# Fewer table loads on ScalarE, silus of a pair of places together, and attention steps of unequal spacing in a macaron block

## The chip, the cores and the metric

The kernel runs on one core of one Trainium2 chip. The core has five engines with an instruction queue each: TensorE (PE in the profile; its weight loads are listed as PEld), VectorE (DVE), ScalarE (ACT), GpSimd (POOL) and SyncE (SP), which here only issues transfers. The metric is the device time of one execution in microseconds (us), lower is better.

## What is computed

Eight sequences of 512 tokens with 512 channels go through half a feed-forward network, attention, and half a feed-forward network again, each behind a layer norm and added to its input:

```
x = x + 0.5 * ffn(layernorm(x), w_gate, w_up, w_down)
x = x + attn(layernorm(x), W_q, W_k, W_v, W_o)
x = x + 0.5 * ffn(layernorm(x), w_gate, w_up, w_down)
```

`ffn` has 2048 hidden channels. Of every four neighbours of `silu(x @ w_gate) * (x @ w_up)`, only the two of largest magnitude are kept; then comes `@ w_down`. `attn` has 16 query heads and 4 key and value heads of 32 channels, with rotary positions on queries and keys, and a softmax over the 512 keys. All of it is in 32-bit floats.

## The kernel before

**Tiles and stages.** The 16 feed-forward blocks (8 sequences, first and second half) are the main stream. Each goes through four chunks `c` of 512 hidden channels, and each chunk through two places (`pair`), one for gate and up of 256 hidden channels. A place is done by `woven`: seven products of half size (Strassen's scheme) in place of eight, named by their PSUM banks x, v and z. Each product is four matmuls in the program and eight in the profile, some 1.73 us of PE (starts 0.216 us apart). Partial results are collected in the SBUF tiles `row` and `corner`; `copied` puts a first partial result there by ACT or by DVE, whichever the planner takes to be free sooner. Silu of the gate part and the multiply by the up part are done for three pieces: the corner (line 634, after the fifth product), the part still in x (line 645) and the row (line 650), both after the last product. Each multiply is recorded as a small task for DVE.

After two places `keep_two_of_four` masks the chunk: `magnitudes` takes the absolute values of one half on ACT (line 371), DVE compares them and multiplies (lines 384 to 409), POOL makes five sums for the products that follow (lines 415 to 420). Those seven products, with the banks y, are `products` (line 523); they are held in `owed` and given out between later places.

**Attention and layer norms are side stages.** They are Python generators. Between two products of the main stream, at most one step of each running side is issued. An attention is 65 steps: the layer norm (loads, moments on DVE, scales on POOL at lines 272 to 280, four `normalise` on ACT at line 283, four transposes), five projections and V, then, for four groups `c` of heads, scores and their maxima (line 805, reduced on DVE), their transpose, and for each of four key tiles `st` and the exponential p (lines 838 to 846), and `ops`, which multiplies p by V (line 854). p is added up over key tiles on DVE; `den` (line 872) sums it over keys, and the reciprocal is made on ACT as exp(-ln(den)) (lines 875 and 877). At the end come four products with W_o (line 932).

**What sets the order.** The schedule is written by the kernel itself: instructions run on each engine in the order in which the Python code records them. A planner keeps an estimated time for PE, DVE and ACT in `at`, and `takes` advances it. DVE tasks wait in three queues (`urgent`, `put_off`, `for_later`), and `fill`, called after a group of matmuls, records those that fit before the estimated time of PE; otherwise it takes a step of the masking. `ensure` records a task that something needs now. A side has a first and a last place, and its steps are due at equal distances between them (`pace`); a step is issued when its due place is past and its `ready` time has come, or it is three places late.

**Tables.** ACT's function tables are loaded by an instruction of their own. The build puts one ahead of an activation whose function isn't in the table that is loaded. `function(f)` runs f on a dummy of one column, so that the load happens there and not in front of the data:

```
    def function(f):
        nc.scalar.activation(dummy[:, 1:2], dummy[:, 0:1], f)
        takes("act", 1.4)
```

It is called for Exp before each p and for Silu after each p, and for Silu after each reciprocal. Ln and the Exp of the reciprocal have no such call, and their loads stand at their own lines.

Of the kernel before, what the change touches and what calls it, by code (L numbers as in the profile page):

```python
# [26 lines left out]
def macaron_block(  # L27
# [98 lines left out]
    ones32 = const.tile([P, HD], FP, name="ones32")  # L126
    nc.vector.memset(ones32, 1.0)
    dummy = const.tile([P, 2], FP, name="dummy")
    nc.vector.memset(dummy, 0.0)

    z = const.tile([P, NT, N_KV, HD], BF, name="z")
    nc.vector.memset(z, 0.0)
# [87 lines left out]
    def copied(dst, src):  # L220
# [5 lines left out]
        nc.vector.tensor_copy(dst, src)  # L226
        return takes("dve", 0.62, pe_heard())

    def function(f):

        nc.scalar.activation(dummy[:, 1:2], dummy[:, 0:1], f)  # L231
        takes("act", 1.4)

    def transposed(parts):

# [111 lines left out]
    def fill(slack=HEARD):  # L347

        while True:
            steps = thin["next"]  # L350
            for queue in (urgent, put_off, for_later):
                if queue and queue[0].fits(slack):
                    queue[0].run()
                    break
            else:
                if not steps or max(at["dve"], steps[1]) + steps[0] > at["pe"] + slack:
                    return
                step()

# [3 lines left out]
    def keep_two_of_four(h, made, sums=None, halves=(0, 1)):  # L363

        thin["halves"] = halves[0]

        def magnitudes(half):
            a = sp.tile([P, 4, HALF], FP, tag="a", name="a")  # L370
            nc.scalar.activation(a, h[:, :, half * HALF : (half + 1) * HALF], AF.Abs)  # L371
            takes("act", 1.06, at["dve"])
            return a

        yield 0.0, at["pe"] + 2.0
        ensure(made)
        a = magnitudes(halves[0])
        for half in halves:
            hh = h[:, :, half * HALF : (half + 1) * HALF]
            yield 0.7, at["act"]  # L380

            m = sp.tile([P, 8, HALF], BF, tag="m", name="m")
            g01, g23, g02, g13, g03, g12, s0, s1 = (m[:, i, :] for i in range(8))
            nc.vector.tensor_tensor(m[:, 0:2, :], a[:, 0:4:2, :], a[:, 1:4:2, :], ALU.is_ge)
            yield 0.72, 0.0
            nc.vector.tensor_tensor(m[:, 2:4, :], a[:, 0:2, :], a[:, 2:4, :], ALU.is_ge)
            yield 0.7, 0.0
            nc.vector.tensor_tensor(g03, a[:, 0, :], a[:, 3, :], ALU.is_ge)
            nc.vector.tensor_tensor(g12, a[:, 1, :], a[:, 2, :], ALU.is_ge)  # L389
            if half != halves[-1]:  # L390
                a = magnitudes(half + 1)

            yield 0.4, 0.0
            nc.vector.tensor_tensor(s0, g01, g02, ALU.add)
            nc.vector.tensor_tensor(s1, g12, g13, ALU.add)
            yield 0.4, 0.0
            nc.vector.tensor_tensor(s0, s0, g03, ALU.add)
            nc.vector.tensor_tensor(s1, s1, g01, ALU.subtract)
            yield 0.4, 0.0
            nc.vector.tensor_tensor(g02, g02, g12, ALU.add)  # L400
            nc.vector.tensor_tensor(g03, g03, g13, ALU.add)
            yield 0.4, 0.0
            nc.vector.tensor_tensor(g02, g23, g02, ALU.subtract)
            nc.vector.tensor_tensor(g03, g03, g23, ALU.add)
            for r, (s, op, n) in enumerate(
                ((s0, ALU.is_ge, 2.0), (s1, ALU.is_ge, 1.0), (g02, ALU.is_ge, 0.0), (g03, ALU.is_le, 1.0))
            ):
                yield 0.36, 0.0
                nc.vector.scalar_tensor_tensor(hh[:, r, :], s, n, hh[:, r, :], op, ALU.mult)  # L409
            if sums is not None:  # L410


                (h11, h21), (h12, h22) = ([h[:, i::2, :HALF], h[:, i::2, HALF:]] for i in range(2))
                if half == 0:
                    nc.gpsimd.tensor_tensor(sums[:, 2], h11, h12, ALU.add)  # L415
                else:
                    nc.gpsimd.tensor_tensor(sums[:, 1], h21, h22, ALU.add)  # L417
                    nc.gpsimd.tensor_tensor(sums[:, 0], h11, h22, ALU.add)
                    nc.gpsimd.tensor_tensor(h12, h12, h22, ALU.subtract)
                    nc.gpsimd.tensor_tensor(h21, h21, h11, ALU.subtract)  # L420
            thin["halves"] = half + 1

    def step():
        us, ready = thin["next"]
        thin["next"] = next(thin["steps"], None)
        takes("dve", us, ready)

    def need(halves):
        while thin["halves"] < halves and thin["next"]:
# [64 lines left out]
    def ffn(b, final, last):  # L494
# [68 lines left out]
        def hidden(h, i, r, cols):  # L563

            n = cols.stop - cols.start
            for m in range(2):
                ps = Bank([P, n], "gu")
                for k in range(ND):
                    w = quarters[(b, final), i, ((Q11, Q12), (Q21, Q22))[r % 2][k // 2]]
                    nc.tensor.matmul(  # L570
                        out=ps.tile, lhsT=w[:, m, k % 2, :], rhs=xT[:, k, cols], start=(k == 0), stop=(k == ND - 1)
                    )
                takes("pe", 3.62 * n / S)
                fill()
                if m == 0:
                    nc.scalar.activation(h[:, r, cols], ps.tile, AF.Silu)
                    ps.free(end=takes("act", 0.6, pe_heard()))
                else:
                    nc.vector.tensor_tensor(h[:, r, cols], h[:, r, cols], ps.tile, ALU.mult)
                    ps.free(end=takes("dve", 0.62, max(pe_heard(), at["act"])))  # L580
                yield n / S

        def woven(h, i, r, last_one):
# [47 lines left out]
            yield 0.5  # L631
            product(x, S3, ts[:, 2], False, end)
            end = add(corner, x, at_corner)
            nc.scalar.activation(h[:, r + 1, HALF:], corner[:, 0, :], AF.Silu)
            takes("act", 0.4, end)
            multiply = partial(nc.vector.tensor_tensor, h[:, r + 1, HALF:], h[:, r + 1, HALF:], corner[:, 1, :], ALU.mult)
            corner_slots.used(later(0.36, multiply, at["act"]))
            yield 0.5
            z = Bank([P, 2, HALF], "z")
            product(z, Q12, b21, True)  # L640
            at_left = add(left, z, 0.0)
            z.free(end=at_left)
            yield 0.5
            product(x, Q22, ts[:, 3], False, end)
            nc.scalar.activation(h[:, r + 1, :HALF], x.tile[:, 0, :], AF.Silu)
            takes("act", 0.38, pe_heard())
            multiply = partial(nc.vector.tensor_tensor, h[:, r + 1, :HALF], h[:, r + 1, :HALF], x.tile[:, 1, :], ALU.mult)
            last_one[:] = [soon(0.36, multiply, at["act"])]
            x.free(last_one)
            nc.scalar.activation(h[:, r, :], row[:, 0, :], AF.Silu)  # L650
            takes("act", 0.62, at_left)
            multiply = partial(nc.vector.tensor_tensor, h[:, r, :], h[:, r, :], row[:, 1, :], ALU.mult)
            last_one += [row_slots.used(later(0.65, multiply, at["act"]))]
            yield 0.5

        def combine_gu(i):
# [83 lines left out]
    def attention(b):  # L740
# [92 lines left out]
        def exponentials(c, t, mT):  # L833

            st = sc_slots.tile([P, N_KV, S], FP, "st")
            p = p_slots.tile([P, N_KV, S], FP, "p")
            for kv, rows in enumerate(heads):
                nc.tensor.matmul(  # L838
                    out=st[:, kv, :], lhsT=kT[rows, t * P : (t + 1) * P], rhs=qT[rows, c, :], start=True, stop=False
                )  # L840
            for kv in range(N_KV):
                rows = slice(kv * HD, kv * HD + 3)
                nc.tensor.matmul(out=st[:, kv, :], lhsT=ones[rows, :], rhs=mT[rows, :], start=False, stop=True)
            takes("pe", 1.45)
            function(AF.Exp)
            nc.scalar.activation(p, st, AF.Exp)  # L846
            end = takes("act", 1.88, max(pe_heard(), p_slots.ready + 0.1))
            function(AF.Silu)
            return p, end

        def weighted(t, ops, p):
# [15 lines left out]
        def divided(c, ops, p, sums):  # L867
# [4 lines left out]
                nc.tensor.matmul(out=den.tile[rows, :], lhsT=ones32, rhs=p[:, kv, :], start=True, stop=True)  # L872
            takes("pe", 1.6)
            rT = w_slots.tile([P, S], FP, "rT")
            nc.scalar.activation(rT, den.tile, AF.Ln)
            den.free(end=takes("act", 1.9, pe_heard()))
            nc.scalar.activation(rT, rT, AF.Exp, scale=-1.0)
            takes("act", 1.95)
            function(AF.Silu)
            made = later(0.65, partial(nc.vector.tensor_tensor, qT[:, c, :], ops, rT, ALU.mult), at["act"])  # L880
            return [acc_slots.used(w_slots.used(made))]

# [68 lines left out]
    normed = {(b, i): {} for b in range(B) for i in range(2)}  # L951
    WIDTH = 7 * NCH + 7 * NCH // 2
    NORM = 5 + 2 * NT
    ATTENTION = NORM + ND + 2 + NT + 1 + ND * (2 * NT + 1) + 1 + NT

    def place(b, i):
# [26 lines left out]
    def start():  # L983
        for side in list(sides):
            first, last, steps, stage, needs, name = side
            if first <= n and needs in past:
                sides.remove(side)
                pace = (last - first) / steps
                running.append({"due": first, "pace": pace, "left": steps, "stage": stage(), "ready": now})
                running[-1]["name"] = name  # L990

    def go_on(side):

        side["left"] -= 1
        side["due"] += side["pace"]
        side["ready"] = next(side["stage"])
        fill()
        if not side["left"]:
# [76 lines left out]
```

## Time and profile before

| what | us |
|---|---|
| median of 3 runs (3311.47 to 3315.4) | 3312.73 |
| the profiled execution | 3314.09 |
| its span, first to last instruction | 3312.3 |
| ACT: exponentials p, 128 of 1.867 | 238.9 |
| ACT: table loads at line 231, 290 of 1.283 | 372.1 |
| ACT: table loads at lines 875 and 877, 32 each | 41.1 and 41.1 |
| ACT: absolute values, 128 of 1.053 | 134.8 |
| DVE: maxima of scores, 512 of 0.683 | 321.6 |
| DVE: sums and quotients of p by line 157, 384 of 0.717 | 254.7 |
| POOL: five kinds of sums after the masking, 62 each | 414.5 |

The span is one execution under the profiler; the medians come from executions without it. A row of a group of instructions gives line, engine, operation, output and inputs with shapes, the count, busy time, mean ns of one, and how long the engine was idle just before them and for whom it waited. A table of waits gives the waiting engine, instruction and line, what it waited for, and the total, the number and the longest wait. In a table of stretches, the figures after each window are its length, the busy times of PE, PEld, DVE, ACT and POOL with counts, the granted clock of PE, the busy share of the DMA engines, and GB/s.

### The profile page before, as it was taken

The numbers are of one execution on the slowest core, as the hardware profiler recorded it, in microseconds if no ns is written. First come the engines' busy times: TensorE is split into PE (matmuls) and PEld (weight loads), VectorE is DVE, ScalarE is ACT, GpSimd is POOL, SyncE is SP. The second block draws the span as 40 slices with busy tenths as digits, with TensorE's granted clock in tenths as the row PEclk, the third lists the DMA queues.
The fourth block names the chain that finished last, engine by engine and source line by source line (L and its number), as shares of the span: only waits on it lengthen the run. The fifth ranks groups of instructions, "written<-read, shape, count | busy, mean of one in ns | idle before, by whom it ended". The sixth has DMA issues, their size and how long they took to land.

```text
span 3312.3 us, 43741 instructions
## 1 busy us (share of the span) xinstructions
PE 3224.5 (97%) x15880; PEld 2322.0 (70%) x15880; DVE 2293.9 (69%) x4949; ACT 1368.8 (41%) x1841; POOL 569.4 (17%) x868
## 2 busy tenths in 40 slices
PE   8899999999999999999999999998999999999999
PEld 6787657765677667766776668765676668765786
DVE  6767865686577775777668865787568765786554
ACT  2222662246424562266324652256425552266221
POOL 0222002210130022111121112120120122101120
PEclk9999999999999999999999999999999999999999
DMA  7563333542344435334453345333533436333451
GB/s 254 186 234 102 109 120 119 175 140 96 116 165 140 131 116 185 127 120 132 142 171 123 121 142 193 128 113 104 189 103 131 140 123 205 100 122 118 138 172 48
DMA packets 249285, 463.21 MB, mean 140 GB/s; under 512 B 24432, under 2 KB 64368, under 8 KB 248304
## 3 DMA queue, kind: packets, MB, share of 16 engines
q1 hardware_dynamic: 249072, 460.42, 42.3%
q8 instruction: 127, 2.08, 0.3%
q14 instruction: 86, 0.70, 0.1%
HBM read 421.53 MB, written 38.80 MB: 139 GB/s over the span
## 4 chain that ended last, share of the span: by engine, by line
PE 84%; DVE 8%; ACT 4%; DMA 2%; issue 1%; POOL 1%; SPq 0%; DVEq 0%; ACTq 0%; POOLq 0%
PE x L594 22%; PE y L523 21%; PE v L594 11%; PE z L594 6%; PE proj L760 4%; PE sc L805 4%; PE ops L854 4%; PE st L838 4%; PE y L932 3%; DMA xn<-x 1%; PE tr L239 1%; PE gu L570 1%; ACT p L846 1%; PE den L872 1%; DVE p L157 1%
## 5 line engine op out<-in xcount | busy, mean ns | idle before, releaser
L594 PE MATMUL x<-ts,w 128*128 128x256 f32 x3000 | 726.3, 385 | 12.0 <-ACT row L224 6.5
L594 PEld LDWEIGHTS x<-ts,w 128*128 128x128 f32 x3000 | 562.1, 191 | 170.9 <-issue 55.7
L523 PE MATMUL y<-wd,h 128*128 128x256 f32 x1984 | 455.8, 384 | 8.2 <-DVE h L409 5.7
L523 PEld LDWEIGHTS y<-wd,h 128*128 128x128 f32 x1984 | 374.1, 191 | 100.7 <-issue 32.6
L157 DVE TENSOR_REDUCE nm<-sc 128x1 f32<-128x512 f32 x512 | 321.6, 683 | 87.9 <-PE sc L805 86.6
L415 POOL TENSOR_TENSOR e<-h 128x512 f32<-128x512 f32 x62 | 89.9, 1450 | 1664.3 <-DVE h L409 1502.8
L231 ACT ACT_TABLE_LOAD x290 | 372.1, 1283 | 5.8 <-PEq L1064 0.7
L523 PE MATMUL y<-wd,e 128*128 128x256 f32 x1488 | 336.9, 381 | 0.6 <-POOL e L417 0.5
L536 DVE SCALAR_TENSOR_TENSOR x<-y,x 128x512 f32<-128x512 f32 x372 | 242.4, 685 | 123.1 <-PE y L523 121.4
L523 PEld LDWEIGHTS y<-wd,e 128*128 128x128 f32 x1488 | 279.5, 190 | 62.9 <-issue 22.3
L846 ACT ACTIVATE p<-st 128x2048 f32<-128x2048 f32 x128 | 238.9, 1867 | 161.8 <-DVE p L157 91.2
L224 ACT COPY row<-x 128x512 f32<-128x512 f32 x166 | 96.9, 584 | 396.9 <-PE x L594 393.4
L157 DVE TENSOR_TENSOR p<-p 128x512 f32<-128x512 f32 x384 | 254.7, 717 | 6.1 <-PE ops L854 6.0
L594 PE MATMUL v<-ts,w 128*128 128x256 f32 x1000 | 241.2, 384 | 4.3 <-DVE w L661 3.7
L594 PE MATMUL z<-xT,w 128*128 128x256 f32 x1000 | 240.2, 383 | 3.8 <-PE tr L239 2.0
L594 PE MATMUL x<-xT,w 128*128 128x256 f32 x1000 | 241.0, 384 | 0.0
L594 PE MATMUL v<-xT,w 128*128 128x256 f32 x1000 | 239.8, 383 | 0.0
L594 PEld LDWEIGHTS v<-ts,w 128*128 128x128 f32 x1000 | 187.9, 191 | 54.4 <-issue 22.4
L594 PEld LDWEIGHTS x<-xT,w 128*128 128x128 f32 x1000 | 186.7, 191 | 55.2 <-issue 27.5
L594 PEld LDWEIGHTS z<-xT,w 128*128 128x128 f32 x1000 | 187.0, 191 | 53.6 <-issue 23.3
L594 PEld LDWEIGHTS v<-xT,w 128*128 128x128 f32 x1000 | 186.7, 190 | 51.2 <-issue 12.2
L371 ACT ACTIVATE a<-h 128x1024 f32<-128x1024 f32 x128 | 134.8, 1053 | 204.4 <-DVE m L389 114.0
(108 smaller groups left out, 4068.8 us busy)
## 6 DMA issues: line engine op xcount, KB each, us to landing
w<-gu SPq DMA_DIRECT2D x472, 256.0 KB, 3.3
w<-in_w_gu SPq DMA_DIRECT2D x394, 256.0 KB, 3.3
wd<-wd SPq DMA_DIRECT2D x155, 512.0 KB, 4.0
wd<-in_w_down SPq DMA_DIRECT2D x124, 256.0 KB, 5.2
x<-x SPq DMA_DIRECT2D x64, 256.0 KB, 2.6
xn<-x SPq DMA_DIRECT2D x64, 256.0 KB, 6.6
x<-in_x SPq DMA_DIRECT2D x32, 256.0 KB, 3.3
gu<-w SPq DMA_DIRECT2D x32, 256.0 KB, 2.6
```

The lines of the kernel that those rows point to most:

```text
L157: self.does()
L231: nc.scalar.activation(dummy[:, 1:2], dummy[:, 0:1], f)
L371: nc.scalar.activation(a, h[:, :, half * HALF : (half + 1) * HALF], AF.Abs)
L523: nc.tensor.matmul(out=y.tile[:, t, :], lhsT=part[:, t * P : (t + 1) * P], rhs=operands[i][:, n, :], start=(n == 0), stop=(n == 3),)
L536: nc.vector.scalar_tensor_tensor(to, y.tile, 0.5 * sign, to, ALU.mult, ALU.add)
L594: nc.tensor.matmul(out=bank.tile[:, m, :], lhsT=lhs[:, m, k, :], rhs=rhs[:, k, :], start=(first and m == 0 and k == 0), stop=(k == 1), ski ...
L760: nc.tensor.matmul(out=ps.tile, lhsT=wa[:, k, col : col + P], rhs=xT[:, k, :], start=(k == 0), stop=(k == ND - 1))
L805: nc.tensor.matmul(out=sc[:, kv, :], lhsT=qT[rows, c, t * P : (t + 1) * P], rhs=kT[rows, :], start=True, stop=True)
L838: nc.tensor.matmul(out=st[:, kv, :], lhsT=kT[rows, t * P : (t + 1) * P], rhs=qT[rows, c, :], start=True, stop=False)
L846: nc.scalar.activation(p, st, AF.Exp)
L854: nc.tensor.matmul(out=ops[rows, :], lhsT=v[:, t, rows], rhs=p[:, kv, :], start=(t == 0), stop=(t == NT - 1))
L932: nc.tensor.matmul(out=y.tile, lhsT=qT[:, k, t * P : (t + 1) * P], rhs=wo[:, k, :D], start=(k == 0), stop=(k == ND - 1))
```

## The change

`function` remembers the last function that it was called for and does nothing when it is called for the same one. The calls for Silu after p and after the reciprocal are gone; there are calls for Silu two products before the silus of a place and just before them, in `hidden` before each silu, and calls for Ln and for Exp in the reciprocal, whose planned costs fall to what the activations alone take. The corner's silu and its multiply move behind those of x and row, and that multiply becomes one of the entries on which the masking waits. The masking's first step becomes ready when its multiplies are done, told by a function instead of a number; the second half's absolute values are recorded two steps later. Some planned ready times get 0.2 or 0.15 us (`HEARD`, `TOLD`) for the signal between engines. An attention's steps are due at distances weighted by kind. No matmul is added or removed.

```diff
-    nc.vector.memset(dummy, 0.0)
+    nc.vector.memset(dummy, 1.0)
...
+    table = [None]
+
     def function(f):
-        nc.scalar.activation(dummy[:, 1:2], dummy[:, 0:1], f)
-        takes("act", 1.4)
+        if table[0] != f:
+            table[0] = f
+            nc.scalar.activation(dummy[:, 1:2], dummy[:, 0:1], f)
+            takes("act", 1.4)
...
-                if not steps or max(at["dve"], steps[1]) + steps[0] > at["pe"] + slack:
+                if not steps:
+                    return
+                ready = steps[1] if isinstance(steps[1], float) else steps[1]()
+                if max(at["dve"], ready) + steps[0] > at["pe"] + slack:
                     return
                 step()
...
-        def magnitudes(half):
+        def magnitudes(half, ready):
             a = sp.tile([P, 4, HALF], FP, tag="a", name="a")
             nc.scalar.activation(a, h[:, :, half * HALF : (half + 1) * HALF], AF.Abs)
-            takes("act", 1.06, at["dve"])
+            takes("act", 1.06, ready)
             return a
 
-        yield 0.0, at["pe"] + 2.0
+        yield 0.0, lambda: when(made)
         ensure(made)
-        a = magnitudes(halves[0])
+        a = magnitudes(halves[0], ensure(made) + TOLD)
         for half in halves:
             hh = h[:, :, half * HALF : (half + 1) * HALF]
-            yield 0.7, at["act"]
+            yield 0.7, at["act"] + HEARD
...
             nc.vector.tensor_tensor(g12, a[:, 1, :], a[:, 2, :], ALU.is_ge)
-            if half != halves[-1]:
-                a = magnitudes(half + 1)
+            taken = at["dve"]
...
             nc.vector.tensor_tensor(s1, s1, g01, ALU.subtract)
+            if half != halves[-1]:
+                a = magnitudes(half + 1, taken + TOLD)
...
     def step():
         us, ready = thin["next"]
+        takes("dve", us, ready if isinstance(ready, float) else 0.0)
         thin["next"] = next(thin["steps"], None)
-        takes("dve", us, ready)
...
                 if m == 0:
+                    function(AF.Silu)
                     nc.scalar.activation(h[:, r, cols], ps.tile, AF.Silu)
...
             end = add(corner, x, at_corner)
-            nc.scalar.activation(h[:, r + 1, HALF:], corner[:, 0, :], AF.Silu)
-            takes("act", 0.4, end)
-            multiply = partial(nc.vector.tensor_tensor, h[:, r + 1, HALF:], h[:, r + 1, HALF:], corner[:, 1, :], ALU.mult)
-            corner_slots.used(later(0.36, multiply, at["act"]))
             yield 0.5
+            function(AF.Silu)
             z = Bank([P, 2, HALF], "z")
...
             product(x, Q22, ts[:, 3], False, end)
+            function(AF.Silu)
             nc.scalar.activation(h[:, r + 1, :HALF], x.tile[:, 0, :], AF.Silu)
...
-            last_one[:] = [soon(0.36, multiply, at["act"])]
+            last_one[:] = [soon(0.36, multiply, at["act"] + HEARD)]
...
-            last_one += [row_slots.used(later(0.65, multiply, at["act"]))]
+            last_one += [row_slots.used(later(0.65, multiply, at["act"] + HEARD))]
+            nc.scalar.activation(h[:, r + 1, HALF:], corner[:, 0, :], AF.Silu)
+            takes("act", 0.4, end)
+            multiply = partial(nc.vector.tensor_tensor, h[:, r + 1, HALF:], h[:, r + 1, HALF:], corner[:, 1, :], ALU.mult)
+            last_one += [corner_slots.used(later(0.36, multiply, at["act"] + HEARD))]
...
             end = takes("act", 1.88, max(pe_heard(), p_slots.ready + 0.1))
-            function(AF.Silu)
             return p, end
...
+            function(AF.Ln)
             nc.scalar.activation(rT, den.tile, AF.Ln)
-            den.free(end=takes("act", 1.9, pe_heard()))
+            den.free(end=takes("act", 0.6, pe_heard()))
+            function(AF.Exp)
             nc.scalar.activation(rT, rT, AF.Exp, scale=-1.0)
-            takes("act", 1.95)
-            function(AF.Silu)
+            takes("act", 0.65)
...
+    WEIGHTS = [0.5] * (NORM + ND + 2) + [0.7] * (NT + 1) + [0.9] * (ND * (2 * NT + 1) + 1) + [0.5] * NT
...
-                pace = (last - first) / steps
+                weights = WEIGHTS if steps == ATTENTION else [1.0] * steps
+                pace = [(last - first) / sum(weights) * w for w in weights]
...
-        side["due"] += side["pace"]
+        side["due"] += side["pace"].pop(0)
```

## The prediction

> **What bounds the kernel now.** I read the page's engine shares first, then the waits of TensorE (PE), then PE's granted clock in chosen stretches, then the time line at the worst waits.
>
> ```profile
> span 3312.3 us, 43741 instructions
> PE 3224.5 (97%) x15880; PEld 2322.0 (70%) x15880; DVE 2293.9 (69%) x4949; ACT 1368.8 (41%) x1841; POOL 569.4 (17%) x868
> PE 84%; DVE 8%; ACT 4%; DMA 2%; issue 1%; POOL 1%; SPq 0%; DVEq 0%; ACTq 0%; POOLq 0%
> L231 ACT ACT_TABLE_LOAD x290 | 372.1, 1283 | 5.8 <-PEq L1064 0.7
> ```
>
> PE is the bound: it idles 3312.3 - 3224.5 = 87.8 us. The 372.1 us of table loads lie on ScalarE (ACT), which is busy 41%. Removing them is worth only what PE waits because of them. The waits of PE from 200 us to the end (ahead of that lie the start and the opening block):
>
> ```profile
> PE ops L854 <- ACT p L846: 18.4, 13, 3.9
> PE st L838 <- DVE nm L157: 8.7, 8, 1.5
> PE x L594 <- ACT row L224: 6.5, 2, 3.2
> PE den L872 <- DVE p L157: 6.2, 8, 2.0
> PE den L872 <- DVE x L536: 4.6, 2, 3.4
> PE tr L239 <- ACT xT L293: 2.9, 1, 2.9
> ```
>
> The columns are total us, times, longest. All lines of this answer sum to 60.5 us, nearly all in attention stages; start, opening and tail hold the other 27, which this change hardly touches. The table of stretches adds a second loss:
>
> ```profile
> 428.30:431.80 3.50, 3.50 (x16) 0.52 (x9) 0.00 (x0) 2.78 (x4) 0.00 (x0) 0.51 0.00 0
> 558.00:561.40 3.40, 3.40 (x9) 2.69 (x9) 0.46 (x1) 1.27 (x2) 1.64 (x9) 0.50 0.00 0
> 800.30:807.20 6.90, 5.97 (x21) 2.45 (x22) 1.89 (x3) 3.85 (x5) 0.00 (x0) 0.51 0.09 32
> 2309.00:2312.40 3.40, 2.89 (x11) 1.08 (x12) 0.36 (x1) 0.89 (x2) 0.00 (x0) 0.51 0.00 0
> 2981.40:2984.80 3.40, 3.20 (x16) 0.72 (x16) 0.00 (x0) 3.11 (x5) 0.00 (x0) 0.51 0.15 58
> 3111.20:3114.60 3.40, 3.40 (x8) 2.77 (x9) 0.63 (x1) 1.43 (x2) 1.78 (x9) 0.50 0.00 0
> ```
>
> The 0.50 or 0.51, third figure from the end, is the granted clock. Each stretch follows a PE wait of 2.4 to 3.9 us and counts as busy, but 24.0 us at half clock do 12 us of work. Three of them (13.8 us) follow waits for ACT's p, two waits for a row copy, one a wait of den.
>
> How ACT causes such a wait is seen at 420 to 428 us, ACT alone:
>
> ```profile
> 420.76 0.60 ACT L875 ACTIVATE rT<-den 128x512 f32<-128x512 f32 x1 [0.29 <-PE den L872]
> 421.38 1.28 ACT L877 ACT_TABLE_LOAD   x1
> 422.67 0.63 ACT L877 ACTIVATE rT<-rT 128x512 f32<-128x512 f32 x1
> 423.32 1.28 ACT L231 ACT_TABLE_LOAD   x1
> 424.61 0.20 ACT L231 ACTIVATE dummy<-dummy 128x1 f32<-128x1 f32 x1
> 424.83 1.28 ACT L231 ACT_TABLE_LOAD   x1
> 426.13 0.20 ACT L231 ACTIVATE dummy<-dummy 128x1 f32<-128x1 f32 x1
> 426.24 1.86 ACT L846 ACTIVATE p<-st 128x2048 f32<-128x2048 f32 x1
> ```
>
> The exponential stands behind a load of silu's table and one of Exp's, 426.24 - 423.32 = 2.9 us, though Exp's table was in place at 422.67 and no silu lies between. PE waits 2.39 us for this p.
>
> **What the Trainium skill says.** "ScalarE: Activation LUTs", What ACT_TABLE_LOAD costs, gives 1283 ns a load and about 1380 ns of drain. The trace agrees with the first (1283 in every row) and shows only the 0.20 us dummy and gaps of some 0.1 in place of the second, so I price a load with dummy at 1.5 us. The same page, Table sets, lists a set with both exp and ln; in the built programs Ln and Exp still have a load each, before and after. "TensorE: Matmul & The Clock Gate", Part 1, says that idling drops the clock to half for about 3.4 us at a time; the stretches above agree. "SBUF — State Buffer", SBUF: two separate sides, says that VectorE (DVE) with two SBUF inputs and GpSimd (POOL) lock each other out; the trace agrees: two sums p<-p, 717 ns each on average, take 3.46 us at 502.70 beside POOL's 1.71 us sums.
>
> **The change part by part.**
>
> *Loads.* In the order of instructions of the two built programs, loads fall from 354 to 216 and dummies from 290 to 216. ACT loses 138 x 1.283 + 74 x 0.203 = 192 us. Exponentials that follow another Exp with no load between go from 0 to 63 of 128, and pairs of loads with no silu between them from 58 to 15. Copies by ACT (rows and corners) rise from 259 to 316, since the planner's ACT is freer: +57 x 0.585 = 33 us on ACT, and some 57 x 0.69 = 39 us off DVE. What PE gets is the wait for p. The work that PE does between st and the ops that needs p (matmuls counted in the order, at 1.73 us for a woven product) is one product in 13 of 128 cases before, 5 after. With the table in place one product nearly covers p: at 436 to 438 us it cost 0.05 us. I leave 3 of the 18.4 us: -15. Of the half clock behind these waits, half of 13.8 us: -7.
>
> *Silus together.* The corner's silu moves behind the other two, its multiply too. ACT waits 403.3 us in 100 times for the corner at L634, at the head of its queue, with copies and exponentials behind it; this goes to the end of the place, where its data are long there. The price: the Abs of a pair starts later by one silu and one multiply, 0.41 + 0.43 us. The sums on POOL and the down products follow a pair's masking several products later, so these cover it; without cover it is 0.84 us for each of 62 pairs. I take +2, bounds -3 and +10. Silu's table is asked for two products ahead; an Exp that slips between costs two loads, the 15 pairs above.
>
> *Abs, HEARD, readiness as a function, the memset's 1.0.* No instruction is added. Abs of a second half is issued two DVE steps later; it waits for DVE's comparisons anyway (114.0 us on ACT in the waits for m L389), so ACT's queue is held less. 0.
>
> *Steps by weight.* Between the same first and last place, the 65 steps of an attention now have weights 0.5 to 0.9, mean 48.3 / 65 = 0.74. Exponential steps stand 0.9 / 0.74 = 1.21 times as far apart, normalising, projections and W_o 0.67 times. The order shows it: den had only one product between it and the last ops in 3 of 32 cases (one cost 4.4 us at 504), now never under two. I put the whole loss at den at 28 us: 13.3 idle plus 15 inside the groups, where eight matmuls start over up to 4.41 us instead of 0.47. Part of it is DVE's backlog and POOL's lock, which stay: half goes, -14. st behind the maxima: one product between in 6 cases before, 4 after: 8.7 to 5, -3.5. The half clock behind den and row copies, 10.2 us, loses 5; a third of it goes, -2.
>
> *Denser front.* Projections one product apart rise from 9 to 21. Each has 2.6 us of DVE work (four of 0.65) against 1.73 + 3.43 us of PE. Normalising stands behind POOL: ACT waited 47.1 us in 13 times at L283 for rs, up to 6.8 us, and row copies queued behind cost PE 3.24 us twice. Nearer steps make that likelier, a freer ACT milder. The trace has no such spacing; from -5 (both row waits go) to +30 (six more), I take +3, for lack of a reason for either end.
>
> Sum: -15 - 7 + 2 - 14 - 3.5 - 2 + 3 = -36.5. The profiled run is 3314.1 (span 3312.3 and 1.8 around it), 1.4 above the median of 3312.7, so 3276 against the median.
>
> **Rivals.**
> (a) *DVE and POOL are the limit:* only the ACT terms come, -22, and the rest balances: 3291. For it: den's and st's waits name DVE, and the lock with POOL is in no plan. Against: 57 fewer DVE copies and wider steps.
> (b) *Nearly all goes:* the 60.5 us of idle, the 15 inside den and the 12 of clock vanish but for 15: -72, 3240. For it: every wait over 2 us after 200 us lies in an attention stage, where all parts of the change act. Against: head, opening and lock remain, and an order of two thousand entries moved brings waits of its own.
> (c) *Waits only move:* the new order has other collisions of equal sum: 3313, within 3306 to 3319. For it: PE has only 2.7% to win.
> (d) *Slower, the norm's queue:* with steps at 0.67 of the spacing, an Identity reaches ACT before POOL has made rs behind its own 6.5 us of sums; ACT is in order, the row copy behind it is late, PE waits 3.24 us and then runs 3.4 us at half clock: 3.24 + 1.7 = 4.9 us. It decides from 36.5 / 4.9 = 7.4 collisions. With 12 (15 norms of two halves give 30 chances): +59 - 36 = +22, 3335. Against: 13 waits of ACT at rs cost PE only two times before.
>
> **How the numbers follow.** Chances: forecast 0.45 (its own range 3262 to 3288), (a) 0.23, (b) 0.15, (c) 0.07, (d) 0.10. A change under 0.2%, some 6.6 us, can't be told from none here. Faster is the forecast, (a) and (b), 0.83; same (c), 0.07; slower (d), 0.10. From 3246 to 3308 I leave out (d), most of (c) and the lower third of (b), about 0.2.
>
> **What would show it.** Right: 216 loads, ACT busy near 1210 us; ops behind p under 5 us; no half clock behind an ops; den's idle under 8 us; PE idle near 60 us. Wrong: rows behind L224 or L283's successors among PE's waits with over 20 us (d); den and st unchanged (a); or y behind h's last mask where Abs came later. If the opening, 0 to 200 us, shifts by over 5 us, my assumption that it is untouched fails.

## The result and the profile after

The changed kernel takes 3262.97 us (median of 5 runs, 3261.19 to 3266.38) against 3315.4 us for the kernel before in the same session. The ratio is 0.9845, with a 95% interval of 0.9833 to 0.9856. The forecast was 3276, with a range of 3246 to 3308: the direction is right, and the gain is 1.4 times the one forecast (51.1 us from span to span against 36.5).

The page of the changed kernel, its span, engine shares, chain by engine and table loads:

```profile
span 3261.2 us, 43693 instructions
PE 3200.0 (98%) x15880; PEld 2316.7 (71%) x15880; DVE 2261.7 (69%) x4892; ACT 1196.7 (37%) x1686; POOL 564.3 (17%) x868
PE 92%; DVE 4%; DMA 2%; ACT 1%; issue 0%; POOL 0%; SPq 0%; DVEq 0%; ACTq 0%
L236 ACT ACT_TABLE_LOAD x216 | 277.1, 1283 | 4.5 <-PEq L1079 0.7
```

ACT is busy 172.1 us less: the loads take 177.1 us less and the dummies 15.0, the copies of rows and corners 33.7 more, and the remaining 13 us are time in which one activation's record overlaps the next one's. That is not the gain. PE idles 61.2 us in place of 87.8, and its busy time falls by 24.5 us with the same 15880 matmuls: after 200 us most of the half clock and nearly all of the spread inside groups of den, both of which count as busy, are gone. ACT's share of the chain falls from 4% to 1%.

PE's waits from 200 us on (total, times, longest):

```profile
PE sc L817 <- DVE nm L157: 6.9, 7, 1.4
PE y L532 <- DVE row L618: 5.7, 2, 3.0
PE x L604 <- DVE corner L618: 5.4, 3, 2.3
PE st L850 <- DVE nm L157: 4.8, 5, 1.4
PE den L883 <- DVE row L618: 3.1, 5, 0.6
PE den L883 <- DVE x L545: 2.8, 2, 1.6
...
PE ops L865 <- ACT p L858: 0.4, 1, 0.4
```

Line numbers are 10 or so higher than before. The first line of before, ops behind p with 18.4 us, is the next to nothing of the last line here. The rows behind ACT (6.5) and the transpose behind xT (2.9) are gone. At the top stand waits that before hardly had: sc for the maxima, y and x for row and corner. All of these are waits for DVE.

The table of stretches for the one half clock that is left after 200 us, in place of six:

```profile
917.30:920.70 3.40, 3.27 (x9) 2.62 (x10) 1.82 (x7) 0.00 (x0) 1.50 (x2) 0.58 0.01 2
```

It follows the 3.0 us wait of y in the list above. The window begins half a us too early, so its clock is a mean of 0.58; the half clock itself runs for 3.41 us from 917.87 us on.

### The profile page after: what moved, and what is told of

Read it like the earlier page. It is cut to its first block, busy times and chain, and to the rows that moved or that the text cites. A ratio compares the mean times of both kernels' runs of the same rounds, so it can differ in the third digit from the quotient of the medians.

```text
span 3261.2 us, 43693 instructions
## 1 busy us (share of the span) xinstructions
PE 3200.0 (98%) x15880; PEld 2316.7 (71%) x15880; DVE 2261.7 (69%) x4892; ACT 1196.7 (37%) x1686; POOL 564.3 (17%) x868
## 4 chain that ended last, share of the span: by engine, by line
PE 92%; DVE 4%; DMA 2%; ACT 1%; issue 0%; POOL 0%; SPq 0%; DVEq 0%; ACTq 0%
PE x L604 25%; PE y L532 23%; PE v L604 12%; PE z L604 6%; PE proj L772 4%; PE sc L817 4%; PE st L850 4%; PE ops L865 4%; PE y L944 3%; PE tr L244 1%; PE gu L579 1%; DMA xn<-x 1%; DVE nm L157 1%; PE den L883 1%; PE vps L797 1%; PE y L562 1%
## 5 line engine op out<-in xcount | busy, mean ns | idle before, releaser
L604 PE MATMUL x<-ts,w 128*128 128x256 f32 x3000 | 721.5, 383 | 10.7 <-DVE corner L618 9.2
L532 PEld LDWEIGHTS y<-wd,e 128*128 128x128 f32 x1488 | 279.7, 190 | 62.3 <-issue 18.7
L224 ACT COPY row<-x 128x512 f32<-128x512 f32 x212 | 124.1, 585 | 392.5 <-PE x L604 392.1
L653 ACT ACTIVATE h<-x 128x256 f32<-128x256 f32 x125 | 47.5, 380 | 558.1 <-PE x L604 525.0
L604 PEld LDWEIGHTS v<-ts,w 128*128 128x128 f32 x1000 | 186.8, 190 | 54.8 <-issue 20.8
L604 PEld LDWEIGHTS z<-xT,w 128*128 128x128 f32 x1000 | 185.8, 190 | 52.6 <-issue 22.9
```

The lines of the kernel that those rows point to most:

```text
L224: nc.scalar.copy(dst, src)
L532: nc.tensor.matmul(out=y.tile[:, t, :], lhsT=part[:, t * P : (t + 1) * P], rhs=operands[i][:, n, :], start=(n == 0), stop=(n == 3),)
L604: nc.tensor.matmul(out=bank.tile[:, m, :], lhsT=lhs[:, m, k, :], rhs=rhs[:, k, :], start=(first and m == 0 and k == 0), stop=(k == 1), ski ...
```

## The experiments

Medians are of 4 to 7 runs. The kernel before, run beside each, had medians of 3314.5 to 3316.7 us.

| run | us | ratio to before, 95% interval |
|---|---|---|
| changed kernel | 3262.97 | 0.9845 (0.9833 to 0.9856) |
| e1_same_order | 3326.82 | 1.0037 (1.0025 to 1.005) |
| e8_ahead_same_order | 3306.13 | 0.9968 (0.9956 to 0.9981) |
| e6_tables_planned | 3290.06 | 0.9924 (0.991 to 0.9937) |
| e2_loads_back | 3295.03 | 0.9942 (0.9929 to 0.9954) |
| e9_no_dummies | 3267.94 | 0.9854 (0.9839 to 0.9869) |
| e4_weights_alone | 3304.24 | 0.997 (0.9959 to 0.9981) |
| e3_equal_steps | 3272.12 | 0.9872 (0.9858 to 0.9885) |
| e5_corner_back | 3267.31 | 0.9856 (0.9843 to 0.987) |
| e11_mask_back | 3267.98 | 0.9854 (0.9841 to 0.9868) |
| e7_scores_wider | 3259.9 | 0.9836 (0.9823 to 0.985) |
| e10_sums_later | 3263.68 | 0.984 (0.9826 to 0.9853) |
| e12_late_8 | 3252.16 | 0.9814 (0.98 to 0.9827) |

### Fewer loads in the order of before

The kernel before, with no dummy emitted and the planner charged as before:

```diff
     def function(f):
-        nc.scalar.activation(dummy[:, 1:2], dummy[:, 0:1], f)
         takes("act", 1.4)
```

> The kernel before with the same planner and the same order on PE, DVE, POOL and SP; only the dummies are gone, so that ACT loads a table where the next data need another one (225 loads in place of 354). Theory (the loads themselves hold up p): ops' waits for p fall from 18.4 us to under 6, the half clock behind them (13.8 us at half) mostly goes, den and st stay: 3288 to 3296, against 3315 before. Rival (loads cost little by themselves, the gain is in the new order and spacing): 3308 to 3316.

It was 12 us slower than before, outside both expectations, with 129 loads fewer. PE's waits from 200 us on:

```profile
PE ops L853 <- ACT p L845: 28.9, 33, 3.7
PE st L837 <- DVE nm L157: 9.3, 10, 1.5
```

The time line of ACT in this kernel tells why:

```profile
441.59 1.28 ACT L633 ACT_TABLE_LOAD   x1 [4.92 <-DVE corner L607]
442.88 0.42 ACT L633 ACTIVATE h<-corner 128x256 f32<-128x256 f32 x1
445.21 1.28 ACT L845 ACT_TABLE_LOAD   x1 [1.91 <-DVE p L157]
446.50 1.88 ACT L845 ACTIVATE p<-st 128x2048 f32<-128x2048 f32 x1
```

and the same place in the kernel before:

```profile
443.88 1.28 ACT L231 ACT_TABLE_LOAD   x1
445.17 0.20 ACT L231 ACTIVATE dummy<-dummy 128x1 f32<-128x1 f32 x1
447.05 1.88 ACT L846 ACTIVATE p<-st 128x2048 f32<-128x2048 f32 x1 [1.67 <-DVE p L157]
```

In brackets stands the idle time ahead of an instruction and what ended it. With a dummy, the wait for DVE's p stands at the exponential, and the load is over by then. Without one, the wait stands at the load, so its 1.28 us come after the wait. In all, ACT idled 77.0 us ahead of the 70 loads at p's line, 70.7 of it for DVE's p. At 35 of the 70 the wait stood ahead of the load, at 8 it was a wait for PE's st and stood behind it, and at 27 there was none. The Trainium skill, "ScalarE: Activation LUTs", Step-by-step: what each stage is for, says that the compiler places a load right before the activation that needs it; the trace agrees, with loads at 441.59 and 445.21 us right before theirs, and adds the side of the wait on which they land. So this run changed two things at once, number and place, and can't price the loads.

The next run keeps the order of before and the 225 loads, but puts each ahead of the waits by a dummy without a charge:

```diff
+    def ahead(f):
+        if table[0] != f:
+            table[0] = f
+            nc.scalar.activation(dummy[:, 1:2], dummy[:, 0:1], f)
+
     def function(f):
-        nc.scalar.activation(dummy[:, 1:2], dummy[:, 0:1], f)
+        if f != AF.Silu:
+            ahead(f)
         takes("act", 1.4)
```

with `ahead(AF.Silu)`, `ahead(AF.Ln)` and `ahead(AF.Exp)` in front of their data.

> The kernel before in its own order on PE, DVE, POOL and SP, with 225 loads at changes of function as in the first same-order run, but each by a dummy ahead of the waits of the next data. Theory (a load without a dummy starts only after the first wait of its activation, so place counts, and the number only when placed ahead): ops' waits for p fall below 10 us, half clock behind ops goes: 3285 to 3300, against 3315 before and 3327 for the same loads without dummies. Rival (the freed ACT time doesn't reach PE in this order): 3308 to 3320.

3306: some 10 us better than before and 21 better than the same number of loads without dummies. The waits of ops for p are below 10 us as the theory had it, and the half clock after 200 us falls from 23.9 to 13.7 us, but the time lies between the two expectations:

```profile
PE ops L864 <- ACT p L856: 9.5, 7, 4.0
PE st L848 <- DVE nm L157: 8.7, 8, 1.5
PE x L602 <- ACT row L224: 6.5, 2, 3.2
PE den L882 <- DVE p L157: 6.2, 8, 2.0
PE den L882 <- DVE x L543: 4.6, 2, 3.4
...
PE ops L864 <- DVE qT L157: 2.9, 2, 1.5
```

The waits of st, row and den are those of before to the tenth: in this order, the loads that went had no part in them. And ops has a new releaser. Where the kernel before waited 2.39 us for p at 428 us, PE waits here (time line, PE):

```profile
429.65 0.64 PE L864 MATMUL ops<-p,v 128*32 128x512 f32 x4 [1.47 <-DVE qT L157]
```

The bank of ops is free only when DVE has made qT from the ops before. Three fifths of this wait passed to what was late next.

### The planner told of it

The kernel before with the table parts of the change alone (cached `function`, its calls and charges as in the change; silus, masking and spacing of before):

> The kernel before with the table parts alone: loads only at a change of function, told to the planner, Silu's and Ln's and Exp's loads ahead of their data; silus, masking and spacing as before (236 loads). Theory: the gain of the loads as in the same-order run plus that of 50 or so copies moved from DVE to ACT: 3280 to 3294. Rival (the planner, thinking ACT free, puts p and ops closer and loses it again): 3300 or more.

3290, in the theory's range: 24.5 us, where the loads in the old order gave 10. Both kernels put their loads ahead of the data, 236 here and 225 there, so the remaining 14 come with the order that the planner makes for a freer ACT. ops waits as long for p as in the old order (9.3 us against 9.5), but its 2.9 us for qT are gone, st falls from 8.7 to 5.3 us, and den's waits fall from 13.3 to 9.0. So this order helps where PE waits for DVE. The copies by ACT (rows and corners), which the theory named, rose from 259 to 286, by half of what it expected; what they give was not measured apart.

The reverse, the changed kernel's order with the loads of before put back on ACT:

```diff
+            reload(AF.Exp)
             nc.scalar.activation(p, st, AF.Exp)
+            reload(AF.Silu)
```

and `reload(AF.Silu)` behind each reciprocal, where `reload` emits the dummy activation with no charge. There are 354 loads again, but 504 dummies, where the kernel before has 290.

> The changed kernel with its order on PE, DVE, POOL and SP, and the loads of the kernel before put back on ACT (a dummy Exp ahead of each p, a dummy silu behind each p and each reciprocal; 354 loads in place of 216). Theory: waits of ops for p come back to 12 to 20 us, with half clock behind the longest: 3278 to 3292, against 3263. Rival (the wider steps cover the loads): 3263 to 3270.

3295, 32 us more than the changed kernel, a little over the theory's range:

```profile
PE st L853 <- DVE nm L157: 14.8, 14, 2.3
PE ops L870 <- ACT p L862: 12.0, 13, 2.4
PE sc L820 <- DVE nm L157: 6.9, 7, 1.4
```

ops gets back 11.6 of its 18 us. The theory had not seen st: 10 us more. The trace shows where it comes from. Nine of the 14 waits are new, and ahead of each of them DVE had last idled for ACT: six times for a copy xT (7.6 us of st's waits), three times for absolute values (1.7). A tenth wait is 0.7 us longer behind a silu. For one of the two longest, DVE in this run and then in the changed kernel:

```profile
779.08 0.69 DVE L157 TENSOR_TENSOR ts<-xT 128x512 f32<-128x512 f32 x1 [7.05 <-ACT xT L301]
```

```profile
772.52 0.69 DVE L157 TENSOR_TENSOR ts<-xT 128x512 f32<-128x512 f32 x1 [2.52 <-ACT xT L298]
```

The copy xT is late behind loads on ACT, the maxima come next in DVE's queue, and st waits 2.3 us for them. There are three more half clocks of 3.4 us. Nearly the same loads, 129 and 138, are worth 10 us in one order and 32 in the other. A part of the 32 may belong to the 288 additional dummies, some 58 us on ACT; that was not split off.

Leaving out the dummies of the changed kernel (its order, 185 loads in place of 216, where the next data need them):

> The changed kernel in its own order on PE, DVE, POOL and SP, without dummies: each load stands where the next data need it (185 loads in place of 216). Theory (place counts more than number): 3270 to 3290 with more waits of ops for p, against 3263. Rival (fewer loads win): 3255 to 3263.

3268, 5 us more, between the two expectations and with an interval that overlaps the changed kernel's. ops waits 4.7 us for p in place of 0.4. So 31 loads fewer bring no gain here. The longer wait points to a cost of place in this order too, but the times alone do not show it.

### The weights

The changed kernel with `weights = [1.0] * steps` for all sides:

> The changed kernel with all steps of an attention at equal distances again. Theory (the weights bring den's and st's share): den's waits and what is lost inside its groups come back, some 17 to 22 us, with st's 3: 3278 to 3290, against 3263. Rival (a freer ACT and fewer copies on DVE bring it): 3263 to 3270.

3272, 9 us more, between the two expectations. Its waits of PE from 200 us on:

```profile
PE ops L865 <- ACT p L858: 8.7, 10, 1.7
PE st L850 <- DVE nm L157: 5.3, 7, 1.5
PE den L883 <- DVE p L157: 4.0, 5, 1.4
```

den loses 8.1 us idle (ahead of the first matmul of its groups) and 10.7 inside its groups (starts spread over more than 0.47 us), against 7.2 and 0.1 with the weights: 11.5 us come back. ops is back at 8.7 us. But sc's 6.9 us, a product of the weights, are absent, which makes the sum small.

The weights alone, added to the kernel before:

> The kernel before with the weighted steps alone. Theory: den and st gain 17 to 23 us, the loads still hold up p, though less often at a distance of one product: 3288 to 3300, against 3315. Rival (weights bring nothing without the freer ACT): 3310 to 3320.

3304, 11 us better and short of the theory. den loses 10.9 idle and 5.3 inside its groups, some 10 us less than before (11.0 and 15.0), and other waits take their place:

```profile
PE x L594 <- DVE row L226: 13.9, 4, 7.0
PE st L838 <- DVE nm L157: 6.9, 9, 1.4
PE den L872 <- DVE x L536: 6.8, 5, 3.2
PE sc L805 <- DVE nm L157: 6.7, 4, 2.0
...
PE ops L854 <- ACT p L846: 0.4, 1, 0.4
```

The last line matters most: with all 354 loads of before in place, ops hardly waits for p any more. The spacing alone ends the wait that the prediction put on the loads. By itself this gives no time: x behind row, 1.9 us before, and sc, which did not wait before, take it back. All of PE's waits after 200 us still sum to 60 us, and the half clock there grows from 23.9 to 27.3 us. What this run gains is what den no longer loses inside its groups.

### Corner and masking

The changed kernel with the corner's silu and multiply back at their old place, `function(AF.Silu)` in front of them:

> The changed kernel with the corner's silu and multiply at their old place, ahead of the place's last two products (253 loads in place of 216). Theory (silus together only save switches and free the head of ACT's queue): 37 more loads and the wait for the corner back in ACT's queue, 3263 to 3270. Rival (it is a main part, since an exponential behind a waiting silu is late): 3275 to 3290.

3267, 4 us more, in the theory's range, though its interval overlaps the changed kernel's. The other run puts back the masking's edits: absolute values of the second half two steps earlier, its ready times by number, and no `HEARD` and `TOLD` in them.

> The changed kernel with the masking's order and ready times as before (absolute values of the second half two steps earlier, first step ready by a number, no HEARD and TOLD in them). Theory, from what tables alone, equal steps and corner back leave over, 3290 - 3272 - 4 = 14 us: 3270 to 3282. Rival, the prediction's price of nothing for these edits: 3260 to 3267.

3268, 5 us more, with an interval that overlaps the changed kernel's: 1 us outside the expectation of nothing and 2 us short of the theory's range, whose 14 us fall. The trace speaks for a real cost: den loses 8.7 us idle and 4.9 inside its groups, 6.3 us more than in the changed kernel, and ACT copies 188 rows in place of 212. From tables alone (3290) to equal steps (3272) it is 18 us, of which these two edits, each undone alone, explain 9. The rest may lie in how the parts act together; it was not split further.

### The waits at the top after the change

sc waits for the maxima seven times. Giving the score steps more room:

```diff
-    WEIGHTS = [0.5] * (NORM + ND + 2) + [0.7] * (NT + 1) + ...
+    WEIGHTS = [0.5] * (NORM + ND + 2) + [0.9] * (NT + 1) + ...
```

> The changed kernel with the weight of the five score steps at 0.9 in place of 0.7. Theory (the new waits of sc for the maxima, 6.9 us in 7 times, come from that weight): they go, 3254 to 3261, against 3263. Rival (a new order has other collisions of equal sum): 3259 to 3270, with sc's waits gone and others in their place.

3260, with an interval that overlaps the changed kernel's, and sc's waits stay at 6.9 us in 7 times: the theory's cause is wrong, whatever the time. In the order of instructions those seven still stand a single product behind the scores before. A side that is over three places late is forced on at every product, whatever its weights (`LATE`), and it is forced before the planner has its data ready. So:

```diff
-    LATE = 3.0
+    LATE = 8.0
```

> The changed kernel with attention steps forced only when 8 places late instead of 3. In the order of the changed kernel, scores stand one product behind the scores before in 7 cases, and st one product behind scores in 4; here in none. Theory (sc's waits of 6.9 us in 7 times and part of st's 4.8 come from steps issued because they are late, before their data are planned to be there): sc's waits go, 3250 to 3258, against 3263. Rival (the steps held back collide elsewhere): 3260 to 3272.

3252, the fastest kernel here, 11 us under the change, with intervals apart. Its waits from 200 us on:

```profile
PE ops L865 <- ACT p L858: 5.3, 4, 1.5
PE x L604 <- DVE corner L618: 4.1, 5, 1.7
PE v L604 <- DVE ts L157: 2.8, 2, 1.4
PE v L604 <- DVE row L618: 1.7, 1, 1.7
```

The waits of sc and of st are gone, and so is every wait over 2 us after 200 us and the half clock behind it. ops gives 5 us back.

In the opening block, two waits for a corner stand at 49 to 79 us. The sums of weights that DVE makes there were asked for two products later:

```diff
-                        if k == 2 and opens and i + 1 < 2 * NCH:
+                        if k == (4 if i else 2) and opens and i + 1 < 2 * NCH:
```

> The changed kernel with the four sums of gate and up weights for the next place, in the opening block, asked for after the place's fifth product in place of its third (from the second place on). Theory (the two waits of 3.7 and 5.7 us for a corner at 49 to 79 us come from DVE standing at its weights' transfer, with half clock behind them): 5 to 12 us less, 3251 to 3258. Rival (the sums then come late for the next place's second product): 3263 to 3275.

3264, no difference. The first wait fell from 3.7 to 2.1 us, and the second rose from 5.7 to 6.5. The half clock of 3.4 us at the first wait is gone, and one of the same length stands at 236 us, where the changed kernel has none. The theory falls as far as the move of these sums goes; what holds up the second corner stays open.

## Why the prediction was right

By its own terms, counted from 200 us to the end in both traces. den is counted as idle before the first matmul of each group plus the spread of starts inside beyond 0.47 us a group, which gives 26.0 us before. The prediction put 28, since 13.3 us of den's waits include some inside the groups, which its 15 counts again.

| term | forecast | measured |
|---|---|---|
| ops behind p | -15 | 18.4 to 0.4: -18.0 |
| half clock, both terms | -9 | 23.9 us at half to 3.4: -10.2 |
| den | -14 | 26.0 to 7.3: -18.7 |
| st behind the maxima | -3.5 | 8.7 to 4.8: -3.9 |
| silus together, denser front | +5 | not measured apart; the rest of 51.1 is about 0 |

All terms erred to the same side, so the sum was 14.6 us short: 3.0 for ops, 1.2 for the clock, 4.7 for den, 0.4 for st, and 5.3 for the two prices. The rest of about 0 hides movement: without ops, st and den, PE's waits after 200 us sum to 20.1 us before and 20.8 after, in other places. The half clock is in part chance: runs e7, e9 and e10 have the same wait of 3.0 us for y at 914 to 921 us, and no half clock behind it; each stretch is worth 1.7 us. What the prediction named as signs of being right came: 216 loads, ops at 0.4 us, no half clock behind an ops, den's idle at 7.2 us, PE idle 61.2 us. Only ACT is busy 1196.7 us in place of 1210, by the overlap above.

**Loads.** The bound was read rightly: of 172 us off ACT, PE got a small part. That ops had one product in only 5 cases after was counted from the order, and the 3 us left for them were too many: they cost 0.4 us in all, so one product covers an exponential whose table is in place. The prediction took this term and the half clock behind it as the price of the loads. The runs show otherwise: ops still waits 9.3 us for p with the tables alone, and only 0.4 with the weights alone and all loads in place. In the old order the loads give 10 us, told to the planner 24.5, and in the new order putting them back costs 32. So the size of this term was nearly right and its cause only in part. The weak step is to price one edit by one wait, when the edit also tells the planner where it has time, and when another edit ends the same wait.

**Weights and den.** The mechanism was right, the size too small. "Half goes" was a guess about POOL's lock and DVE's backlog. The count of one-product distances (3 before, none after) said more: the spread inside the groups went from 15.0 to 0.1 us. Of the 18.7 us, equal steps bring back 11.5; 6 go with the tables alone, where den loses 7.2 and 12.9.

**Silus together and the masking's edits.** Here the signs look wrong. The silus were charged 2 us, and undoing them costs 4; the masking's edits were put at nothing, and undoing them costs 5. Both are below the 6.6 us under which the prediction would not tell a change from none. For the masking the trace names a place, den's 6.3 us; for the silus it is open.

**Denser front.** Its +3 had a mechanism, ACT's queue behind the norm, which did not come: row's 6.5 us behind ACT are gone, though ACT still waits 51.2 us in 17 times for rs. The denser front has a price of another kind, sc's 6.9 us, from steps that are forced when late. That was seen nowhere in the prediction.

**Rivals.** (a), DVE as the limit at 3291, falls: den and st gained 22.6 us, more than ops. The result lies between the forecast and (b), 3240. With `LATE` at 8 the kernel is at 3252, which bears out its reason, that every long wait after 200 us lay within the reach of such edits; the opening block and head, 23.8 us of PE idle in the first 200 us, stay as forecast (22.9 before). (d) falls, and so does (c) as a whole, though 20 us of waits did only move.

## What to carry to other kernels

In this kernel, whose order is written out by a planner, the edit that frees an engine was worth little until the planner knew it (10 us, then 24.5), and cost much when the planner believed it and it wasn't so (32). Price such an edit in both orders. Apply each part alone as well: here the spacing ended a wait that seemed to belong to the table loads, and as much waiting came up elsewhere until the other parts were there too. Look for distances, the work of the bound engine between a producer and its consumer, and count how many are shorter than the producer needs: here these counts told more than the busy shares. A rule that forces late work on without asking whether its data are ready makes waits of its own, and is cheap to try.

## What the runs showed of the hardware

A table load without an activation of its own can land behind a wait of the activation that needs it: in e1_same_order 77.0 us of ACT's idle time stood ahead of 70 loads of 1.28 us, at 35 of them, and 8 others had their wait behind them. With a dummy of 0.20 us in front, in e8_ahead_same_order, the load stood ahead of the wait, and the same 225 loads took 21 us less.

A small DVE instruction beside POOL's sums can take nearly as long as one of those. In the kernel before, on sixteen columns (DVE's time line):

```profile
2300.77 0.20 DVE L818 CAST z<-nm 128x16 bf16<-128x16 f32 x1
2301.00 1.17 DVE L820 TENSOR_TENSOR nm<-nm,z 128x16 f32<-128x16 f32 x1
2302.21 1.20 DVE L821 CAST z<-nm 128x16 bf16<-128x16 f32 x1
2303.45 1.17 DVE L820 TENSOR_TENSOR nm<-nm,z 128x16 f32<-128x16 f32 x1
2304.65 0.20 DVE L821 CAST z<-nm 128x16 bf16<-128x16 f32 x1
```

Four sums of 1.26 to 1.28 us ran on POOL from 2299.62 us on. Each of the three long ones ended some 0.05 us after the sum that ran when it began. The other 62 of the 64 instructions of L820 took 0.2 us. Of the casts, with one input, the one at 2302.21 us was held up, and the one at 2300.77, begun near the end of a sum, was not.
